# Four-layer kernel, layer 3: expert groups finish their tokens and scatter rows to the output, and blank slots are written behind the tokens

## The chip, the cores and the metric

The kernel runs on one core of a Trainium2 chip. The metric is the device time of one execution in microseconds (us); the figure used is the median of the runs shown. Engine names: PE is TensorE (matmul; PEld its weight loads), DVE is VectorE, ACT is ScalarE, POOL is GpSimd, SP is SyncE, which here only issues DMAs. "Idle" and "busy" are those of the profile.

## What is computed

The input is 32 sequences of 256 tokens with 128 numbers each: 8192 tokens, which the kernel holds as 64 tiles of 128 tokens (one token a partition). Four layers of "x = x + mixer(norm(x))" and "x = x + feed-forward(norm(x))" follow. The change concerns mainly the last line of the last layer, and with it the slots that layer 1 uses too:

```python
# layer 1: 8 experts, 2 a token, hidden size 512, gelu, plus one shared expert
# layer 3, feed-forward part (x is the normed stream, 8 experts, one a token, hidden size 256)
attn_out = mha(x)                                   # 16 heads of 8
x = layernorm(x + attn_out, ln1_g, ln1_b)
gp = softmax(x @ w_group + b_group)                 # group of experts
ep = softmax(x @ w_expert[group] + b_expert)        # expert in the group
moe = (g_prob * e_prob) * (relu(x @ w1[e] + b1[e]) @ w2[e] + b2[e])   # e: the one expert picked
x = layernorm(x + moe, ln2_g, ln2_b)
# and the stream's own residual around all of it: out = stream + x
```

## The kernel before, in words

**Stages in order of time.** Layer 0 (to about 830 us), layer 1 with its mixer, router and shared expert (to 1200), layer 1's routed experts (to 1490), layer 2's attention (to 2090), `middle` (layer 2's feed-forward and layer 3's recurrent mixer, to 2260), layer 3's attention with its router beside it (to 2831, router and scatter to 2877), layer 3's routed experts (to 3017), and a last pass over all tokens (to the end).

**Slots.** A token that goes to an expert is put into a slot, a row in device memory. `Slots` (L304) gives each of 8 experts room for 8192 + 256 rows. A row is `WIDE` = 130 numbers: 128 of x, the row that its result belongs to (column D), and its weight (column D + 1). `send` (L476) is one indirect DMA on POOL for a tile of 128 tokens: row i goes to the slot that the router counted out. Experts work on groups of 256 slots, and there are always `tokens / 256 + 8` groups (72 in layer 1, 40 in layer 3), so slots without a token are also read. For these `fill` (L324), called in layer 0 (L962), writes all 67,584 rows of each layer with blanks, in 176 DMAs on POOL, each after an iota that gives a blank slot a row of its own to put its result in. The tensor `back` therefore has a row for each slot, and behind them one for each token.

**The expert stage.** `experts` (L489) is a hand-made pipeline: PE, ACT, DVE and SP run in the order in which the code issues instructions, and POOL takes its own in order too. For each group g the loop issues `rise(g)` (first matmul and the activation of group g), `fetch(g + 1)` and `fall(g - 1)`.
- `fetch`: SP reads the group's first slot into a register (L509) and loads 256 rows (`xs`, L513); DVE reads the expert number (L516), copies that expert's weights and bias (L520, L522), casts the column of places (L524), PE transposes the rows (L527), DVE copies the result out of PSUM (`xT`, L529).
- `rise`: PE makes `hp` (L538), ACT the activation `h` (L544).
- `fall`: PE makes `o` (L552, L557), DVE multiplies by the weights (`y`, L563), and POOL scatters 2 tiles of 128 rows to `back` by indirect DMA (L484).

The tiles `xs`, `place`, `b2`, `xT` and `y` have 4 buffers each, `w` and `h` have 3. `place` and `y` are free again when the scatter that reads them has landed.

**Layer 3 around it.** The tile `row` (L2352) holds all 64 tiles of layer 3 for the whole layer, 130 numbers a token; `middle` borrows its memory as scratch. `attention` (L1643) works on 32 sequences b in 4 steps each (step t, 128 steps plus a lead of 7 and an end of 4), in the order written in `step`. `rows(b)` (L2420) writes the normed input of sequence b, 4 sequences ahead; `done(b)` (L2581) takes the statistics of the attention's sum and adds the last norm's offset to `K.x`. Every 8 tiles (`CHUNK`, 4 sequences) a generator `settle` (L2434) applies the norm, on POOL except for the last chunk; `gate` (L2453) transposes a pair of tiles and makes its router logits, once in 4 steps (`t % TURNS == 2`), and at each step from 128 on; `choose` (L2489) picks the expert, counts out slots (`places`, L378) and sends 8 tiles. `beside` advances each generator by one step, twice in a step t; only the oldest `choose` moves. After the last step `more(None)` runs what is left. `finish` (L434) works out the expert and first slot of each group.

**The last pass** (L2631 to L2665). In four quarters of 16 tiles: SP loads results from `back` (L582), DVE adds them (L2639) and takes statistics (L246), `Norm.steps` (L252, 19 small DVE instructions) closes the norm, ACT applies mean and scale (L2648), DVE multiplies by the norm's gain (L2655), POOL adds the stream (L2656), SP writes the output (L2657).

Of the kernel before, what the change touches and what calls it, by code (L numbers as in the profile page):

```python
# [11 lines left out]
F32 = mybir.dt.float32  # L12
# [8 lines left out]
P = 128  # L21
# [203 lines left out]
class Norm:  # L225
# [18 lines left out]
    def take(self, src, lo, hi):  # L244
        for j in range(lo, hi):
            self.nc.vector.bn_stats(self.st[:, j, :], src[:, j, :])  # L246
# [57 lines left out]
class Slots:  # L304
# [8 lines left out]
    GROUP, WIDE, NE = 256, D + 2, 8  # L313
    ROOM = NT * P + GROUP

    def __init__(self, K, es, tag, ranks):
        self.K, self.tag, self.ranks = K, tag, ranks
        self.groups = ranks * NT * P // self.GROUP + self.NE
        self.count = self.NE * self.ROOM
        dram = K.pool(es, tag + "slots", 1, DRAM)  # L320
        self.rows = dram.tile([self.count, self.WIDE], F32, name=f"{tag}_rows")
        self.back = dram.tile([self.count + ranks * NT * P, D], F32, name=f"{tag}_back")

    def fill(self, pool):  # L324
        nc = self.K.nc
        n = 6
        blank = [pool.tile([P, n, self.WIDE], F32, name=f"blank{i}") for i in range(2)]
        for t in blank:
            nc.gpsimd.memset(t, 0.0)
        rows = self.rows.rearrange("(c p n) w -> c p n w", p=P, n=n)  # L330
        for i in range(self.count // P // n):
            t = blank[i % 2]
            nc.gpsimd.iota(  # L333
                t[:, :, D], pattern=[[1, n]], base=i * n * P, channel_multiplier=n,
                allow_small_or_imprecise_dtypes=True,
            )
            nc.gpsimd.dma_start(rows[i], t)  # L337

    def begin(self, pool, most):

        nc = self.K.nc
        self.every = pool.tile([P, P], BF16, name="every")
# [28 lines left out]
    def belongs(self, row, j, n, rank):  # L371

        self.K.nc.gpsimd.iota(
            row[:, j : j + n, D], pattern=[[P, n]], base=self.count + (rank * NT + j) * P,
            channel_multiplier=1, allow_small_or_imprecise_dtypes=True,
        )

# [56 lines left out]
    def finish(self, pool, long, expert, start):  # L434
# [16 lines left out]
        past = pool.tile([1, n, NE - 1], F32, name="past")  # L451
        nc.vector.tensor_tensor(
            past, self.number.unsqueeze(2).to_broadcast([1, n, NE - 1]),
            end[0:1, 0 : NE - 1].unsqueeze(1).to_broadcast([1, n, NE - 1]), ALU.is_ge,
# [3 lines left out]
        nc.vector.tensor_scalar(expert, which, float(long), None, ALU.mult)  # L458
# [3 lines left out]
            past, past, need[0:1, 0 : NE - 1].unsqueeze(1).to_broadcast([1, n, NE - 1])  # L462
# [20 lines left out]
    def result(self, place, row):  # L483
        i = self.K.nc.gpsimd.indirect_dma_start(  # L484
            self.back, bass.IndirectOffsetOnAxis(ap=place, axis=0), row, None
# [3 lines left out]
    def experts(self, w_all, expert, start, F, act):  # L489
# [9 lines left out]
        with ExitStack() as ps:  # L499
            gp = K.pool(ps, tag + "g", 4)  # L500
            wp = K.pool(ps, tag + "gw", 3)
# [5 lines left out]
            def fetch(g):  # L507
# [4 lines left out]
                xs = gp.tile([P, N, self.WIDE], F32, name="xs")  # L512
                nc.sync.dma_start(  # L513
                    xs, self.rows[bass.ds(at, self.GROUP)].rearrange("(n p) w -> p n w", p=P)
                )
                at = nc.vector.value_load(  # L516
# [6 lines left out]
                place = gp.tile([P, N], mybir.dt.uint32, name="place")  # L523
                nc.vector.tensor_copy(place, xs[:, :, D])  # L524
# [4 lines left out]
                nc.vector.tensor_copy(xT, t)  # L529
# [19 lines left out]
            def fall(g):  # L549
# [12 lines left out]
                y = gp.tile([P, N, D], F32, name="y")  # L562
                nc.vector.tensor_mul(y, o, xs[:, :, D + 1 : D + 2].to_broadcast([P, N, D]))  # L563
                for i in range(N):
                    self.result(place[:, i : i + 1], y[:, i, :])

            with K.tc.manual_schedule(
                engines={nc.tensor.engine, nc.scalar.engine, nc.vector.engine, nc.sync.engine}
            ):
                for g in range(-1, self.groups + 1):  # L570
# [4 lines left out]
                    if g > 0:  # L575
                        fall(g - 1)

    def results(self, pool, n, eight):

        back = self.back[self.count :].rearrange("(r j p) d -> r p j d", r=self.ranks, p=P)  # L580
# [331 lines left out]
def l0_ffn(K):  # L912
# [4 lines left out]
    with ExitStack() as es:  # L917
# [44 lines left out]
        for slots in (K.slots1, K.slots3):  # L962
            slots.fill(sp)
# [675 lines left out]
RING = 4  # L1639
# [1139 lines left out]
```

## Time and profile before

| what | value |
|---|---|
| median of 4 runs | 3089.6 us (3083.45 to 3095.86) |
| the profiled execution, its own time | 3094.01 us |
| its span, first to last instruction | 3092.3 us |
| busy: PE, DVE, ACT, POOL | 2492.2, 1853.7, 1424.5, 854.4 us |
| layer 3's experts, first load to last scatter | 2877.0 to 3018.5 us |
| scatters of results (L484) | 224, 958 ns each (median) |
| scatters of rows (L478) | 192, 958 ns each (median) |
| blank DMAs (L337) and iotas (L333) | 176 each, 557 and 136 ns (median) |

The profile is of one execution. Its chain of waits follows the work that ended last back to its releaser. A row of groups names line, engine, operation, output and input, count, busy time, mean of one, then idle time before it and what ended that. "SPq" and "DVEq" are the instruction queues' own work, such as issuing a DMA or loading a register.

### The profile page before, as it was taken

To read this page: it belongs to the slowest core of one execution; us is meant where nothing else is said; L and a number is where in the kernel's file an instruction comes from. 1 tells how busy PE (TensorE), PEld (TensorE's weight loads), DVE (VectorE), ACT (ScalarE), POOL (GpSimd) and SP (SyncE) were. 2 spreads that over 40 slices of the span, in tenths; PEclk is the share of its full clock that TensorE was granted. 3 is DMA by queue.
4 is the path that set the end of the run, shared out by engine and by line. 5 is a ranking of instruction groups with operands and counts; after the bars stand their busy time and mean duration, and the time that the engine had idled before them with its cause. 6 is when DMAs were issued, how large, how long until landed. Compare 5 with 4: busy or idle time off the path is not lost.

```text
span 3092.3 us, 59293 instructions
## 1 busy us (share of the span) xinstructions
PE 2492.2 (81%) x21486; PEld 1848.1 (60%) x21486; DVE 1853.7 (60%) x5498; ACT 1424.5 (46%) x3065; POOL 854.4 (28%) x1235
## 2 busy tenths in 40 slices
PE   4899778899797953999489989997978888886670
PEld 4865444445766742999466767766755555564560
DVE  7215444445877312444389767755879988886347
ACT  3423432222387521444345555556337776664223
POOL 1001444310012455455311001000620234334553
PEclk9999889999898986999779999996979999998795
DMA  2497455530001111222455444420044445440324
GB/s 71 142 283 221 180 237 225 223 131 18 12 1 56 39 42 51 70 70 70 121 159 160 126 126 140 137 61 12 1 117 133 137 126 142 125 140 28 90 74 112
DMA packets 263264, 340.81 MB, mean 110 GB/s; under 512 B 34598, under 2 KB 231062, under 8 KB 254780
## 3 DMA queue, kind: packets, MB, share of 16 engines
q1 hardware_dynamic: 231228, 237.01, 26.8%
q0 software_dynamic: 27584, 97.92, 8.4%
q8 instruction: 170, 2.79, 0.4%
q10 hardware_dynamic: 4160, 2.10, 0.3%
q14 instruction: 122, 1.00, 0.1%
HBM read 156.72 MB, written 177.83 MB: 108 GB/s over the span
## 4 chain that ended last, share of the span: by engine, by line
PE 39%; DVE 11%; issue 7%; DMA 5%; POOL 5%; ACT 5%; SPq 1%; another core or an unknown queue 0%; POOLq 0%; ACTq 0%; DVEq 0%
PE o L1909 6%; PE t L1888 5%; PE hp L538 4%; PE o L557 4%; DVE top L1845 4%; DMA q<-row 3%; PE s L1784 2%; PE s L1833 2%; POOL f_back L484 2%; PE a L1592 2%; PE d L1607 2%; ACT e L1896 2%; DVE st_x L246 1%; POOL f_rows L478 1%; PE a L1492 1%
## 5 line engine op out<-in xcount | busy, mean ns | idle before, releaser
L1845 DVE TENSOR_REDUCE top<-s 128x3 f32<-128x384 f32 (+1 forms) x1024 | 600.3, 617 | 177.6 <-PE s L1742 122.6
L1896 ACT ACTIVATE e<-t 128x384 f32<-128x384 f32 (+1 forms) x1024 | 493.8, 546 | 121.6 <-PE s L1742 78.7
L1888 PE MATMUL t<-q,k 64*128 64x256 f32 (+1 forms) x2048 | 421.3, 310 | 108.7 <-ACT e L1896 62.3
L1833 PE MATMUL s<-k,q 48*128 48x256 f32 (+1 forms) x2048 | 441.6, 333 | 28.4 <-DMA k<-d 16.1
L1888 PEld LDWEIGHTS t<-q,k 64*128 64x128 f32 x2048 | 303.2, 193 | 188.8 <-ACT e L1896 91.1
L1833 PEld LDWEIGHTS s<-k,q 48*128 48x128 f32 x2048 | 311.3, 200 | 42.0 <-DVE top L1845 22.6
L544 ACT ACTIVATE h<-hp,w 128x256 f32<-128x256 f32 x368 | 154.4, 471 | 356.5 <-PE hp L538 304.5
L484 POOL DMA_INDIRECT f_back<-y,place x224 | 216.8, 968 | 216.1 <-DVE y L563 146.3
L1909 PE MATMUL o<-e,val 128*32 128x256 f32 (+1 forms) x4096 | 260.2, 374 | 0.0
L538 PE MATMUL hp<-xT,w 128*128 128x256 f32 x736 | 188.9, 397 | 30.2 <-DVE xT L529 23.2
L557 PE MATMUL o<-w,h 128*128 128x128 f32 x1472 | 187.6, 280 | 0.0
L557 PEld LDWEIGHTS o<-w,h 128*128 128x128 f32 x1472 | 178.5, 197 | 1.8
L2079 POOL TENSOR_SCALAR xn<-x_sb,mean_x,r_x 128x128 f32<-128x128 f32 x64 | 55.1, 869 | 441.3 <-PE t L1773 386.4
L538 PEld LDWEIGHTS hp<-xT,w 128*128 128x128 f32 x736 | 135.9, 197 | 50.6 <-DVE xT L529 27.1
L1909 PEld LDWEIGHTS o<-e,val 128*32 128x32 f32 x4096 | 110.2, 112 | 81.1 <-issue 11.2
L1742 PE MATMUL s<-hideq,pick 64*128 64x128 bf16 x1024 | 153.1, 235 | 0.0
L478 POOL DMA_INDIRECT f_rows<-row,one x128 | 123.3, 963 | 101.9 <-DVE one L1422 67.6
L1742 PE MATMUL t<-hidek,pick 64*128 64x128 bf16 x1024 | 148.7, 229 | 0.0
L527 PE MATMUL t<-ident,xs 128*128 128x128 f32 x224 | 45.4, 286 | 105.3 <-DMA xs<-f_rows 105.3
L563 DVE TENSOR_TENSOR y<-o,xs 128x256 f32<-128x256 f32 x112 | 47.4, 423 | 129.6 <-PE o L557 116.2
L337 POOL DMA_DIRECT2D f_rows<-blank x176 | 98.4, 559 | 54.5 <-POOL blank L333 51.2
L775 PE MATMUL up<-wc,hT 128*128 128x128 f32 x768 | 110.8, 297 | 0.0
(522 smaller groups left out, 5297.3 us busy)
## 6 DMA issues: line engine op xcount, KB each, us to landing
f_rows<-blank POOLq DMA_DIRECT2D x176, 390.0 KB
tz<-kpad SPq DMA_DIRECT2D x64, 512.0 KB
d<-high SPq DMA_DIRECT2D x128, 256.0 KB
d<-low SPq DMA_DIRECT2D x128, 256.0 KB
q<-d SPq DMA_DIRECT2D x128, 256.0 KB
k<-d SPq DMA_DIRECT2D x128, 256.0 KB
xs<-f_rows SPq DMA_DIRECT2D x112, 130.0 KB
t<-f_back SPq DMA_DIRECT2D x24, 512.0 KB
```

The lines of the kernel that those rows point to most:

```text
L478: i = self.K.nc.gpsimd.indirect_dma_start(self.rows, bass.IndirectOffsetOnAxis(ap=slot, axis=0), row, None)
L484: i = self.K.nc.gpsimd.indirect_dma_start(self.back, bass.IndirectOffsetOnAxis(ap=place, axis=0), row, None)
L538: nc.tensor.matmul(hp[:, i, :], w[:, (c + i) * P : (c + i + 1) * P], xT, start=True, stop=True,)
L544: nc.scalar.activation(h[:, c + i, :], hp[:, i, :], act, bias=w[:, b1 : b1 + 1])
L557: nc.tensor.matmul(o[:, i, :], h[:, c, i * P : (i + 1) * P], w[:, F + c * D : F + c * D + D], start=False, stop=i == N - 1 and c == FC - 1,)
L775: nc.tensor.matmul(o, hT[:, 2 * blk + b, s : s + P], wc[:, j, cs], start=j == 0, stop=False)
L1742: nc.tensor.matmul(t.rearrange("p (n q) -> p n q", n=3)[:, 0:3:2, 64 * n : 64 * n + 64], pick[r, n, :], hide[name][r], start=False, stop=n ...
L1833: nc.tensor.matmul(s[:, lo:hi], q[r, p, h * P : (h + 1) * P], k[r, p, 0 : hi - lo], start=h == 0, stop=not causal and h == 1,)
L1845: nc.vector.tensor_reduce(tops[b][:, :, j, p], out_of["s"][:, 0:used].rearrange("q (h k) -> q h k", h=3 if causal else 2), axis=AX.X, op=A ...
L1888: nc.tensor.matmul(t[:, kh * SEQ : kh * SEQ + SEQ - skip], k[r, p, kh * P : (kh + 1) * P], q[r, p, skip:SEQ], start=kh == 0, stop=not caus ...
L1896: nc.scalar.activation(e, t, AF.Exp)
L1909: nc.tensor.matmul(o[32 * i : 32 * i + 32, skip:SEQ], val[b % RING][:, kh, 4 * m + i, 16 * s : 16 * s + 32], e[:, kh * SEQ : kh * SEQ + SE ...
```

## The change

- A slot row of layer 3 has 258 numbers: the token's normed x, the stream's row with the last norm's offset already added, place and weight. Layer 1's rows stay at 130. `row` becomes a ring of 18 tiles of two token tiles each, one a sequence.
- Expert groups of layer 3 finish their tokens in a new `leave`: product with the weight plus x, statistics, and, for four groups at a time, the norm's closing, its application, gain and sum with the stream; then the row is scattered straight to the kernel's output. Work is metered: 11 units an iteration, 1 for a small DVE instruction, 5 for a group. The last pass is gone.
- `xs`, `place` and the new result tile have 12 buffers in layer 3 (4 in layer 1 as before). In layer 3 the copy `xT` moves from DVE to ACT.
- `fill` is gone. `begin` writes one blank group, and `blanks` writes 256 blank rows behind each expert's last token (SP reads the position from a tile into a register). A blank's place lies outside the output, and the scatter leaves out places that are out of bounds. The first group's load waits for the blank writes.
- One group fewer in both layers (71 and 39).
- Layer 3's `gate` runs every second step; `middle` has a scratch tile of its own.

The core of the diff:

```diff
 class Norm:
+    def take(self, src, lo, hi, at=None):   # statistics of src[at...] to column lo...
 class Slots:
-    GROUP, WIDE, NE = 256, D + 2, 8
+    GROUP, NE = 256, 8
+        self.PLACE, self.WEIGHT, self.WIDE = width, width + 1, width + 2
-        self.groups = ranks * NT * P // self.GROUP + self.NE
+        self.groups = self.tokens // self.GROUP + self.NE - 1
...
+    def put_blank(self, at):
+        i = self.K.nc.sync.dma_start(
+            self.rows[bass.ds(at, self.GROUP)].rearrange("(n p) w -> p n w", p=P), self.blank
+        )
+    def blanks(self, pool):
+        nc.vector.tensor_copy(last, self.seen[0:1, :])
+        for e in range(self.NE):
+            self.put_blank(
+                nc.sync.value_load(
+                    last[0:1, e : e + 1], min_val=0, max_val=self.count - self.GROUP
+                )
+            )
...
     def result(self, place, row):
-            self.back, bass.IndirectOffsetOnAxis(ap=place, axis=0), row, None
+            self.back, bass.IndirectOffsetOnAxis(ap=place, axis=0), row, None,
+            bounds_check=self.tokens - 1, oob_is_err=False,
...
     # experts(..., leave, keep, copy)
+            kp = K.pool(ps, tag + "gk", keep)
-                xs = gp.tile([P, N, self.WIDE], F32, name="xs")
+                xs = kp.tile([P, N, self.WIDE], F32, name="xs")
-                nc.vector.tensor_copy(xT, t)
+                copy(xT, t)
-                y = gp.tile([P, N, D], F32, name="y")
-                nc.vector.tensor_mul(y, o, xs[:, :, D + 1 : D + 2].to_broadcast([P, N, D]))
-                for i in range(N):
-                    self.result(place[:, i : i + 1], y[:, i, :])
+                leave(g, o, xs, place)
...
 def l0_ffn(K):
-        for slots in (K.slots1, K.slots3):
-            slots.fill(sp)
...
 def layer1(K):   # in choose, after places; leave there is the old product and two scatters
+            if hi == NT:
+                S.blanks(rw)
...
 def l3_ffn(K):
+                row_of[b] = kept.tile([P, 2, S.WIDE], F32, name="row")   # kept: 18 buffers
-                nc.vector.reciprocal(row[:, lo:hi, D + 1], low)
+                for j in range(lo, hi, 2):
+                    two = row_of[j // 2]
+                    nc.vector.reciprocal(two[:, :, S.WEIGHT], low[:, j - lo : j - lo + 2])
+                    S.belongs(two, j, 2, 0)
-                two = K.x[:, 2 * b : 2 * b + 2, :]
-                nc.gpsimd.tensor_add(two, two, spread(2, 3))
+                nc.gpsimd.tensor_add(
+                    row_of[b][:, :, D : 2 * D], K.x[:, 2 * b : 2 * b + 2, :], spread(2, 3)
+                )
-                if t % TURNS == 2 or t >= NB * TURNS:
+                if t % 2 == 0 or t >= NB * TURNS:
...
+            def out_of(g, j, r, xs, place):
+                for i in range(2):
+                    nc.scalar.activation(
+                        r[:, i, :], r[:, i, :], AF.Identity, bias=nmr[:, j + i : j + i + 1],
+                        scale=first.r[:, j + i : j + i + 1],
+                    )
+                nc.vector.tensor_mul(r, r, spread(2, 2))
+                nc.gpsimd.tensor_add(r, r, xs[:, :, D : 2 * D])
+                for i in range(2):
+                    S.result(place[:, i : i + 1], r[:, i, :])
+            def work(groups):
+                lo, hi = groups[0][1], groups[-1][1] + 2
+                for _ in first.steps(lo, hi):
+                    yield 1
+                nc.vector.scalar_tensor_tensor(
+                    nmr[:, lo:hi], first.mean[:, lo:hi], -1.0, first.r[:, lo:hi], ALU.mult, ALU.mult
+                )
+                yield 1
+                for group in groups:
+                    out_of(*group)
+                    yield 5
+            def leave(g, o, xs, place):
+                if g is not None:
+                    j = g // BATCH % SETS * tiles + 2 * (g % BATCH)
+                    r = yp.tile([P, 2, D], F32, name="r")
+                    for i in range(2):
+                        nc.vector.scalar_tensor_tensor(
+                            r[:, i, :], o[:, i, :], xs[:, i, S.WEIGHT : S.WEIGHT + 1],
+                            xs[:, i, 0:D], ALU.mult, ALU.add,
+                        )
+                        nc.vector.bn_stats(first.st[:, j + i, :], r[:, i, :])
+                    batch.append((g, j, r, xs, place))
+                if batch and (g is None or g % BATCH == BATCH - 1 or g == S.groups - 1):
+                    todo.append(work(batch[:]))
+                    batch.clear()
+                most = 11 if g is not None else 1000
+                while todo and most > 0:
+                    done = next(todo[0], None)
...
+            S.experts(w_all, expert, start, F, AF.Relu, leave, 3 * BATCH, nc.scalar.copy)
-        # the last pass: results, join, close, end
```

## The prediction

> **What bounds the kernel now.** I read the slices first, then the waits stage by stage, then the chain from 2840 us on, and last the timeline of single groups. The windows around the change (PE, PEld, DVE, ACT, POOL busy; granted clock; DMA share; GB/s):
>
> ```profile
> 2264.00:2831.00 567.00, 479.46 (x4958) 324.36 (x4958) 480.11 (x1366) 377.03 (x836) 161.64 (x212) 0.95 0.44 125
> 2831.00:2877.00 46.00, 6.55 (x30) 5.37 (x30) 23.65 (x123) 6.54 (x34) 23.25 (x24) 0.50 0.28 81
> ...
> 2888.00:3017.50 129.50, 96.81 (x577) 83.58 (x575) 54.64 (x188) 31.86 (x76) 76.85 (x79) 0.91 0.27 78
> 3017.50:3092.30 74.80, 0.00 (x0) 0.00 (x0) 57.29 (x168) 25.06 (x64) 26.86 (x17) 0.50 0.41 114
> ```
>
> In the attention (567 us) PE and DVE are each 85% busy. From 2831 to 2877 nearly everything waits. In the experts' 129.5 us no engine is full (PE 75%, POOL 59%, DVE 42%). In the last 74.8 us PE has nothing to do: this pass stands alone at the end. The chain of waits says what holds these stretches:
>
> ```profile
> 2873.37 0.96 POOL f_rows L478
> 2874.33 14.00 issue
> ...
> 2990.01 1.27 issue
> 2991.51 0.96 POOL f_back L484
> ...
> 3019.81 4.12 DMA t<-f_back
> ...
> 3073.87 11.07 POOL x_sb L2656 x7
> ```
>
> The experts hang on POOL's scatters, and still POOL idles: one scatter is 0.96 us and 0.30 us to the next, so two are 2.52 us a group, while 40 groups took 129.5 us, 3.24 each. The waits of 2886 to 3017 us name the missing part: places waiting for scatters to land, POOL waiting for the product.
>
> ```profile
> POOL f_back L484 <- DVE y L563: 44.2, 18, 14.2
> ...
> DVE place L524 <- DMA f_back<-y,place: 16.1, 7, 3.7
> ```
>
> This is the ring of 4 places and products: the product of one group waits for a landing, the next scatter waits for the product.
>
> **Part 1, the last pass goes into the groups.** I count DVE per group, from starts in the timeline:
>
> ```profile
> 2920.08 0.43 DVE L520 COPY w<-w_all 128x514 f32 x1 [0.45 <-issue]
> 2920.42 0.22 DVE L522 CAST b<-w_all 128x128 bf16 x1
> ...
> 2924.14 0.16 DVE L524 CAST place<-xs 128x2 uint32<-128x2 f32 x1
> ```
>
> - Weights 0.34 to the next start, bias 0.13, place 0.17: 0.64. Before the weights DVE loads the expert's register: a gap of 0.43 typically (0.10 where its queue ran ahead); I take 0.43. The copy `xT` (0.42) goes to ACT.
> - Two products with sum, 128x128: L1562, the same instruction in layer 1, means 344 ns, 0.68. Two statistics: eight take 1.65 us (L246), 0.42.
> - The closing of a norm: 20 instructions, 3029.76 to 3033.70, 3.94 us; once per four groups, 0.99 each. The gain: L2447 on DVE, 128x256, 0.43 and a step of 0.03: 0.46.
> - Sum 3.62 us. Waits on ACT: after the closing, two Identities (64 in 25.1 us, 0.39 each) and two hand-overs before the first gain, 1.0 us; the three other gains follow ACT's 0.78 instead of 0.46, 1.0 more. Two per batch, 0.50 each: 4.1.
> - The gain against POOL's addition: L2655 (128x512) takes 684 ns at its fastest and 1660 at the median, with POOL adding beside it. The addition fills 0.72 of some 4 us, so I add 0.1: **c = 4.2 us a group**.
>
> [...] If each group's gain met the addition of the group ahead and waited half of it, 0.36 instead of 0.1, the sum below would be 9 us longer.
>
> The other engines stay under 4.2: POOL 2 x 1.26 + 0.72 (L2585, the same addition of 128x256) + 0.06 = 3.3; PE 2.36 (start to start of transposes, 2891.27 and 2893.63); ACT 2 x 0.42 + 0.37 + 0.78 = 2.0. Twelve buffers instead of four take away the wait for landings: a place waits for the scatter 12 groups back, and POOL has at least 4 groups queued then. So what is late next is DVE, in its own order. SP is queued behind nothing new here; a load is 0.9 us of its queue (L509 and L513: 0.27 + 0.15 + 0.02 + 0.04 + 0.03 + 0.38), and rows of 264 KB instead of 130 come 12 groups ahead.
>
> The stretch from the first load of slots to the end of the span is 3092.3 - 2877.0 = 215.3 us now. After: 10.9 us to the first product (2877.0 to 2887.9, PE cold, unchanged); three more groups with no work given out, 2.6 each (PE's 2.36, a little slower at the start), 7.8; 35 groups at 4.2, 147.0; then the last batch: nine closing steps 1.9, Identities and gain 1.5, POOL's three groups 9.9, the last landing 2.3 (3017.51 to 3019.81) and 1.4 to end, 17.0. Together 182.7: **-32.6**.
>
> Ends for c: 3.3, POOL's sum, if DVE's waits vanish; 5.2, if PE runs cold (below). An output row lands like a row of `back` now: both are 512 bytes.
>
> **Part 2, the stretch before.** `gate` twice as often finishes a chunk's logits 8 steps earlier (4 pairs in steps 30 to 36 instead of 30 to 42, the fifth gate at 38 instead of 46). So the sixth chunk's sends, 2834.80 to 2844 now, fall into the attention; the seventh's `choose` starts at about 2831 instead of 2836; the last one no longer waits for it until 2853.84 but starts when its logits are there, 2849.80. From there to slots took 6.7 us, then eight sends at 1.26: the last ends at 2867 instead of 2874.3, -7.4. But now SP writes blanks: eight register loads and DMAs at 0.95, 7.6 us, from when all tokens are counted (2859.4 now, about 2855.4 then), sharing its queue with the 17 weight loads (2855.9 to 2864.5); and the first slots wait for these 2.1 MB. That ends at 2870 to 2874, as a load lands in 2.1 us (2876.99 to 2879.09), against 2877.0 now. I take **-5**; from -7.4 to +5, if the weights queue behind the blanks.
>
> **Part 3, the attention.** The first `rows` now stand at 2209 us, before `middle` ends. The ring lies over `middle`'s memory, so they wait for its last matmul, as `xT` does today (2258.82, released by L2324): four Identities at 0.45 and a transpose on the way, **+3** (0 to 4). The ring itself: a sequence's row is sent at steps 49 to 52 of its chunk's count and overwritten at step 56, 4 to 7 steps of 4 us later; a scatter lands in 2.3. No stall. 24 more reciprocals on DVE, 0.16 to 0.20 each, 4.3 us on an engine that is 85% busy: **+3** (0 to 5). 32 iotas (0.14) and no more additions than before lie on POOL, 29% busy here; rows of 1032 bytes instead of 520 leave POOL's 0.96 a send as it is, or double it at worst: for the last eight sends alone +8.
>
> **Part 4, elsewhere.** Layer 1 has one group fewer, at 3.84 us (1484.92 to 1481.08, PE-bound): **-3.8**. Its scatters go the new bounded way: 2.52 of 3.84 us, hidden at today's price. The 176 blank DMAs and their iotas take 122 us of POOL and most of the DMA traffic of 340 to 640 us, but in 320 to 700 us only one compute wait of note names a DMA, `xn` L991 for 9.6 us, and it ends at 340.17, when DVE finishes `nmr` at 340.0 anyway. So **0**, from -5 to 0. Two small blank fills at the layers' starts (0.4 us of POOL, one DMA issue) hide behind DVE's norm and bias splitting.
>
> **Sum**: -32.6 - 5 + 3 + 3 - 3.8 = -35.4. The profiled execution took 3094.0 (span 3092.3 and 1.7 around it), 4.4 over the median; I take the difference from the median: 3089.6 - 35.4 = **3054**.
>
> **Rivals.**
> 1. *PE goes cold and DVE's order tightens* (0.17). While DVE closes a norm, ACT stands at the Identity, and the next `h` behind it on ACT waits; PE then runs out. For: after 2.43 us idle PE's four matmuls took twice as long:
>
> ```profile
> 2913.22 2.08 PE L538 MATMUL hp<-xT,w 128*128 128x256 f32 x4 [2.43 <-DVE xT L529]
> ...
> 2916.91 1.03 PE L538 MATMUL hp<-xT,w 128*128 128x256 f32 x4
> ```
>
> Against: it recovered by the next group, and PE may run a group ahead. A cold group is 4.7 us; with hand-overs c = 5.0 gives -7.4: 3082. [...]
> 2. *POOL sets the pace* (0.12): ACT and DVE hide each other's waits, c = 3.3: -35.4 - 35 x 0.9 = -67: 3023. For: POOL would hold some groups of work ahead, so DVE's waits cost it nothing; against: DVE's bare sum is already 3.6.
> 3. *The bounded scatter is dearer, slower* (0.08). No row has one. At x us each, layer 1 is POOL-bound above 1.92, and 71 (2x - 3.84) + 35 (2x + 0.78 - 4.2) reaches the 35.4 gained at x = 2.02. At 2.2 it is slower by 39: 3129. For: 1792 or so blank rows a layer have to be left out; against: the work per row is a comparison.
> 4. *The ring of 18 stalls ACT* (0.04): if sends fell back to today's step 57, after the overwrite at 56, each of 14 sequences would wait some 4.5 us: +63, 3117.
>
> That the last pass remains in some form is excluded by the code.
>
> **Chances.** My forecast (c from 3.6 to 4.8, 3033 to 3075) has 0.59, rivals 0.17, 0.12, 0.08 and 0.04. About 0.5% (15 us) is what a measurement can tell from no change. Faster by more: forecast, rival 2 and a little of rival 1: 0.73. Within: the rest of rival 1, 0.14. Slower: rivals 3 and 4 and the far end of 1, 0.13. The range leaves out rivals 3 and 4 and the ends of 1 and 2: 3024 to 3088.
>
> **What would show it.** Right: no DVE or POOL work after the last `o` but some 17 us; in the expert stage DVE over 80% busy, 4.2 us between transposes, no place waiting for a scatter; `f_rows` loads from about 2874; the bounded scatter at 0.96 us. Wrong: `hp` at twice its length in most groups; POOL above 90% there; a scatter above 1.9 us in layer 1; ACT waiting for `f_rows` in the attention; a stage before 700 us that got shorter.

## The result, and the profile after

The changed kernel took **3079.8 us** (median of 44 runs, 3065.0 to 3097.1), the kernel before 3086.8 on the same chips (70 runs, 3071.1 to 3100.9); the ratio is 0.9974 [0.9964, 0.9983]. The sign was forecast, the size was not: -7.0 us by the medians, instead of -35.4. The profiled execution after took 3081.93, its span 3080.2, 12.1 less than the span before.

The same windows as before, with ends set by the same events (columns: PE, PEld, DVE, ACT, POOL busy; granted clock; DMA share; GB/s). The third is two full batches of the experts, the fourth begins with the last `o`:

```profile
2264.00:2831.00 567.00, 494.85 (x4960) 334.15 (x4960) 483.25 (x1392) 376.81 (x842) 164.62 (x241) 0.94 0.45 129
2831.00:2882.50 51.50, 6.38 (x30) 5.25 (x29) 21.16 (x117) 4.23 (x24) 20.91 (x22) 0.52 0.44 141
2928.00:2963.00 35.00, 21.69 (x120) 18.73 (x120) 27.30 (x105) 14.86 (x41) 22.54 (x25) 0.89 0.32 92
3048.00:3080.20 32.20, 1.29 (x8) 1.04 (x8) 9.53 (x35) 5.70 (x15) 18.68 (x21) 0.55 0.06 17
```

The last pass with 74.8 us of no PE work is gone; 32.2 us remain, and POOL is the busy engine in them. DVE is 78% busy in the experts (27.30 of 35; the sign asked for over 80%), POOL 64%. But the stretch of waiting after the attention has grown, from 46.0 to 51.5.

The account, step by step, with ends read from the timelines. The rows on `rows` and on the attention are means over all profiles with the one code or the other in that stage (four before, but three for the attention, where `b_gate2` has code of its own, and thirteen after), since single executions scatter there by 4 to 8 us; the others are of the pair of profiles. (In that pair alone the attention ends 0.7 us later after, where the first three rows add up to 5.8; hence 12.1 between the two spans and 7.0 between the medians.)

| step | forecast | measured |
|---|---|---|
| layer 1, one group fewer (first to last `hp`, 275.1 to 271.2) | -3.8 | -3.9 |
| `rows` waits for `middle` (last addition of layer 2 to first of layer 3, 237.9 to 239.6) | +3 | +1.7 |
| layer 3's attention (first to last addition of the joined stream, 498.8 to 506.8) | +3 | +8.0 |
| Part 2, last addition to first load of slots (47.0 to 51.8) | -5 | +4.8 |
| Part 1, first load to the end of the span (215.3 to 197.7) | -32.6 | -17.6 |
| stages without the fill | 0 | not to be told from 0 (below) |
| sum | -35.4 | -7.0 |

So the 28.4 us that are missing lie in three places: 15.0 in Part 1, 9.8 in Part 2 and 3.7 in the attention and its start. Part 1 once more, by its own terms:

| | forecast | measured |
|---|---|---|
| first load to the end of the first `o` | 10.9 | 11.6 |
| to the end of the last `o`, 38 intervals | 154.8 | 155.9 |
| end of the last `o` to the end of the span | 17.0 | 30.2 |

**The pace was right, the end was not.** The timeline of the end of the experts:

```profile
3048.68 1.29 PE L588 MATMUL o<-w,h 128*128 128x128 f32 x8 [0.86 <-ACT h L575]
3048.81 0.68 POOL L2699 TENSOR_TENSOR r<-r,xs 128x256 f32<-128x256 f32 x1 [3.76 <-DVE r L2698]
...
3049.77 1.00 POOL L501 DMA_INDIRECT out<-r,place  x1 [0.28 <-POOL r L2699]
...
3061.76 0.71 POOL L2699 TENSOR_TENSOR r<-r,xs 128x256 f32<-128x256 f32 x1
...
3070.42 0.98 POOL L501 DMA_INDIRECT out<-r,place  x1 [0.30 <-issue]
```

When PE makes the last product, POOL only begins the batch before it: four groups with eight scatters, 3048.81 to 3061.76, 12.95 us. Then come the last three groups, 9.64 us to 3071.40, which the forecast had (9.9), and 8.8 us to the end of the span. The last closing and its Identities (forecast 1.9 and 1.5) lie hidden beside the work on those four groups. POOL's closing step, a DRAIN in the profile, takes up nearly all of the 8.8; its rows after, and then before:

```profile
L2845 POOLq DRAIN  x3: 51/116/11945, 3067.5 to 3079.9; - x3
L2845 SPq DRAIN  x3: 7/7/7, 3072.8 to 3079.7; - x3
L2775 POOLq DRAIN  x3: 46/116/7528, 3084.0 to 3092.0; - x3
```

Columns are shortest, median and longest in ns, first and last start. SP, which waits for the last data, begins to close at 3072.8; POOL's long step begins at 3067.5, lasts 11.9 us and so ends at 3079.4, 8.0 us after its last scatter. In before the same step ended 5.4 us after POOL's last instruction, an addition.

**The rhythm behind it**, in the chain of waits through the experts (start, length, what):

```profile
2937.34 0.98 POOL out L501
...
2940.96 3.67 issue
...
2958.20 4.21 issue
```

Here POOL has emptied its queue and waits, once a batch (17.35 us for four groups, 4.35 a group). It waits because DVE closes the norm only behind the fourth product, and it gets four groups at once:

```profile
2943.05 0.17 DVE L2707 SCALAR_TENSOR_TENSOR nmr<-mean_x,r_x 128x8 f32<-128x8 f32 x1
2943.25 0.88 ACT L2694 ACTIVATE r<-r,nmr,r_x 128x128 f32<-128x128 f32 x2 [5.47 <-DVE nmr L2707]
...
2944.16 0.43 DVE L2698 TENSOR_TENSOR r<-r,b_f_ln 128x256 f32<-128x256 f32 x1 [0.94 <-ACT r L2694]
...
2944.67 0.67 POOL L2699 TENSOR_TENSOR r<-r,xs 128x256 f32<-128x256 f32 x1 [3.72 <-DVE r L2698]
...
2945.78 1.75 PE L569 MATMUL hp<-xT,w 128*128 128x256 f32 x4 [3.21 <-DVE b L553]
```

POOL works 13.6 us and idles 3.7. In the body its idle time costs nothing, since DVE sets the pace; but the batch is handed on so late that its whole work is still to do when the next batch's products end.

**The stretch before the experts.** The chain of waits there:

```profile
2860.66 0.71 issue
2861.39 0.71 SPq L375
2862.09 0.70 issue
2862.82 0.71 SPq L388
2863.52 0.70 issue
2864.24 0.70 SPq L375
...
2874.12 0.37 SPq L375
2874.53 0.27 SPq L388
2874.85 0.15 SPq L388
2875.26 0.37 SPq L375
...
2876.83 0.47 SPq L2677
...
2882.50 2.62 DMA xs<-f_rows
```

SP writes the blanks (L375 issues the DMA, L388 loads the register). From 2860.66 each of its small steps, or the pause ahead of it, takes 0.70 us, and only at 2872.7 do they return to 0.37 and less, some 3 us after the last scatter of rows began (2869.61). The eight blanks take 15.4 us instead of the forecast's 7.6, and 8 of the 17 weight loads queue behind them, from 2876.83.

### The profile page after: what moved, and what is told of

The parts are those of the page before. It is cut to its first block, busy times and chain, and to the rows that moved or that the text cites. A ratio compares the mean times of both kernels' runs of the same rounds, so it can differ in the third digit from the quotient of the medians.

```text
span 3080.2 us, 59477 instructions
## 1 busy us (share of the span) xinstructions
PE 2513.2 (82%) x21444; PEld 1865.2 (61%) x21444; DVE 1872.4 (61%) x5663; ACT 1437.0 (47%) x3112; POOL 739.4 (24%) x933
## 5 line engine op out<-in xcount | busy, mean ns | idle before, releaser
L1930 PE MATMUL t<-q,k 64*128 64x256 f32 (+1 forms) x2048 | 427.5, 312 | 93.5 <-ACT e L1938 45.5
L569 PE MATMUL hp<-xT,w 128*128 128x256 f32 x724 | 190.2, 404 | 51.6 <-DVE b L553 32.3
L495 POOL DMA_INDIRECT f_rows<-row,one x192 | 185.9, 968 | 181.0 <-DVE one L1451 67.1
L501 POOL DMA_INDIRECT f_back<-y,place x142 | 141.4, 996 | 143.5 <-DVE y L1665 99.7
L1951 PEld LDWEIGHTS o<-e,val 128*32 128x32 f32 x4096 | 110.6, 113 | 82.0 <-issue 12.9
L551 DVE COPY w<-w_all 128x1028 f32 (+1 forms) x110 | 74.1, 674 | 67.8 <-DVE y L1665 29.2
L558 PEld LDWEIGHTS t<-ident,xs 128*128 128x128 f32 x220 | 33.2, 152 | 126.2 <-issue 115.3
```

The costliest lines, as they stand in the source:

```text
L495: i = self.K.nc.gpsimd.indirect_dma_start(self.rows, bass.IndirectOffsetOnAxis(ap=slot, axis=0), row, None)
L501: i = self.K.nc.gpsimd.indirect_dma_start(self.back, bass.IndirectOffsetOnAxis(ap=place, axis=0), row, None, bounds_check=self.tokens - 1, ...
L569: nc.tensor.matmul(hp[:, i, :], w[:, (c + i) * P : (c + i + 1) * P], xT, start=True, stop=True,)
L1930: nc.tensor.matmul(t[:, kh * SEQ : kh * SEQ + SEQ - skip], k[r, p, kh * P : (kh + 1) * P], q[r, p, skip:SEQ], start=kh == 0, stop=not caus ...
L1951: nc.tensor.matmul(o[32 * i : 32 * i + 32, skip:SEQ], val[b % RING][:, kh, 4 * m + i, 16 * s : 16 * s + 32], e[:, kh * SEQ : kh * SEQ + SE ...
```

## The experiments

Marks used below: "stretch" is the last addition of the attention to the first load of slots (before 47.03, after 51.82), "body" the first to the last `hp` (before 130.2, after 158.7), "tail" from there to the end of the span (81.7 and 35.2), "stage" first load to end (215.3 and 197.7). Each ratio is to the kernel before, run in turn on the same chip. `a_fill3_again`, `b_gate2` and `c_nofill` ran on a chip on which the kernel before took 3096.0 us, so their times compare with others only by the ratio. Stretch, body, tail and stage are of one profile each.

**The ring, in the kernel before (`b_keep12`).** Three pools get 12 buffers in layer 3:

```diff
+            kp = K.pool(ps, tag + "gk", 12 if self.ranks == 1 else 4)
-                xs = gp.tile(...); place = gp.tile(...); y = gp.tile(...)
+                xs = kp.tile(...); place = kp.tile(...); y = kp.tile(...)
```

> The kernel before with one edit: in layer 3's expert stage the tiles xs, place and y have 12 buffers instead of 4. Theory (the step of part 1 that says a ring of 4 places and products holds POOL back): 40 groups go from 3.24 us to POOL's two scatters, 2.52 to 2.6 us, so the stage is 25 us shorter and the time some 3062 us. Rival (the product comes late for another reason, the chain of copy, product and activation through DVE, ACT and PE): the pace stays near 3.2 us and the time near 3087 us.

3086.1 us, ratio 1.0003 [0.9982, 1.0024]; 3.22 us a group, 3.32 in the kernel before. Its longest waits in the experts:

```profile
ACT h L545 <- PE hp L539: 37.2, 16, 3.5
POOL f_back L484 <- DVE y L564: 22.5, 13, 2.3
```

No place waits for a landing any longer, POOL's wait for the product has halved (44.2 before), and the pace is the same within the scatter (body 126.3 for 130.2; in `b_gate2`, with these groups unchanged, 124.0). "This is the ring of 4" falls: the wait was there, but it did not hold the pace.

**The same with `xT` on ACT (`b_keep_xT`)**: `nc.scalar.copy` at L529 as well.

> The kernel before, with 12 buffers for xs, place and y in layer 3 (which alone changed nothing: 3.22 us a group instead of 3.32) and the copy xT on ACT as in the changed kernel. Theory (DVE's order is what holds the groups: the copy xT stands behind weights, bias and place and ahead of the product): the pace falls to 2.6 us, POOL's two scatters, and the time by some 20 us to 3065. Rival (the loop of PE and ACT, or stalls that no engine explains): the pace stays above 3.0 us and the time within 5 us of before.

3085.1 us, 0.9997 [0.9976, 1.0017], body 130.05. So neither the ring nor DVE's copy held the old experts; what does stays open. Of the change it says that the deeper rings, alone or with `xT` moved, bring nothing.

**Blanks filled early again (`a_fill3`, and a second time `a_fill3_again`).** Layer 3's slots are filled in layer 0 by 88 DMAs from one constant tile, nothing is written behind the tokens:

```diff
+    def fill(self, pool): ...; for i in range(self.count // P // n): nc.gpsimd.dma_start(rows[i], blank)
+        K.slots3.fill(sp)
-                if hi == NT:
-                    S.blanks(rw)
```

> The changed kernel, but layer 3's slots are filled with blanks in layer 0 (88 DMAs on POOL, 70 MB, all with a place outside the output), and no blanks are written behind the tokens of layer 3. Theory (SP's eight register loads and blank writes, with half the weights queued behind them, set the start of the experts): the first slots load at 2873.5 to 2875 us instead of 2882.5, the time falls by 8 us against the changed kernel. Rival 1 (the start hangs on the router's last scatters and the weights themselves): no change, within 2 us. Rival 2 (the fill in layer 0 is not free): 5 us or more are lost before 830 us.

> The kernel with the fill in layer 0 once more, since its trace had 10.6 us less ahead of the experts than the changed kernel and its median only 3. If the trace is right, the median is now 3067 to 3071; if the fill costs something ahead of 2830 us that one profile can't show, 3075 to 3078 again.

3076.7 us, 0.9962 [0.9946, 0.9979], and 3078.9, 0.9938 [0.9917, 0.9959]. The stretch is 41.2 and 41.1: 10.6 shorter than after, 6 shorter than before. The first load comes 2.9 us after the last scatter of rows, where after has 12.9. So in the profiles the blanks behind the tokens cost 10.6 us of the stretch. The times show less of it: by the ratios 4 us and 11 us below after, the first not clear of noise. The second run's 3078.9 is what its expectation gave for a fill that costs something elsewhere, but by the ratio, on the median of the kernel before, it would be 3068, which is what the profile says; layer 1 starts no later with the fill (below).

**What slows SP.** Three kernels were run once, one in turn with the kernel before. `a_nosend` fills early, writes the blanks too and leaves out the last chunk's eight scatters (its tokens don't reach the experts). `a_now` loads only expert 0's weights and the biases, three loads (the other experts' are zeros; the expectation's count of ten is a slip). `a_wact` issues the weights from ACT. `a_wfirst` puts the blanks behind all weight loads on SP.

```diff
# a_nosend
-                    S.send(one, row(j))
+                    if hi < NT: S.send(one, row(j))
# a_now
+            nc.gpsimd.memset(w_all[:, :, 0 : 2 * F], 0.0)
-            for e in range(NE):
+            for e in range(1):
# a_wact
-                nc.sync.dma_start(w_all[:, e, 0:F], ins["f3_w1"][e])
+                nc.scalar.dma_start(w_all[:, e, 0:F], ins["f3_w1"][e])
# a_wfirst: S.blanks moved behind the loop of loads
```

> The changed kernel, with layer 3's slots also filled in layer 0, and without the last chunk's eight scatters of rows (these 1024 tokens are left out). For the 0.70 us that each SP instruction takes ahead of and among the blank writes. Theory 1 (POOL's scatters of rows slow SP while they run): SP goes at its usual pace, the eight blanks take 9.3 us instead of 15.4. Theory 2 (the weights' traffic) and theory 3 (first use of these instructions after a long time): 0.70 us each remain for 9 to 12 us.

> The changed kernel, loading the first product's weights of one expert only, and all second products' weights (the other experts' first weights are zeros that POOL writes, some 4 us more on POOL ahead of its scatters). Theory 2 (weights in flight on SP's queue slow its other instructions): with ten loads instead of 17 and five of the nine ahead of the blanks gone, the stretch of 0.70 us instructions shrinks by half or vanishes. Theories 1 and 3: it stays, and by theory 1 it ends some 3 us after the last scatter of rows, wherever that is.

> The changed kernel with layer 3's 17 weight loads issued on ACT's queue instead of SP's. So far SP's instructions took 0.70 us each only where the weights were loaded on SP and rows were scattered by POOL at once: not without the last scatters, and not with 3 loads instead of 17. If SP's own loads are what matters, SP goes at its usual pace here: eight blanks in 9.3 us, and from the attention's last addition to the first slots load 51.8 us become 43 to 46. If the traffic matters whoever issues it, the 0.70 us steps remain and it stays over 49.

> The changed kernel with layer 3's blanks issued on SP after the 17 loads of the weights instead of after 9 of them. Theory (order on SP's queue: the weights' second half waits behind the blanks, whose register instructions take 0.7 us each for 12 us): the weights are issued by 2864 us, the blanks then end at 2874 to 2877 and the first slots load at 2876 to 2879 instead of 2882.5: the time falls by 4 to 6 us. Rival (the slow SP instructions are due to the place behind a long wait, so they only move): the blanks end at 2881 and nothing is gained, within 2 us.

SP's row of the eight blanks in the timeline of each (start, time from the first to the last one's end). After:

```profile
2861.39 15.40 SPq L375 DMA_DIRECT2D f_rows<-blank  x8
```

`a_nosend`, no last scatters:

```profile
2863.16 8.54 SPq L385 DMA_DIRECT2D f_rows<-blank  x8
```

`a_now`, three loads:

```profile
2850.14 8.78 SPq L375 DMA_DIRECT2D f_rows<-blank  x8
```

`a_wact`, loads issued by ACT:

```profile
2849.83 17.29 SPq L375 DMA_DIRECT2D f_rows<-blank  x8
```

`a_wfirst`, blanks last on SP:

```profile
2865.21 9.28 SPq L375 DMA_DIRECT2D f_rows<-blank  x8
```

Without the scatters the blanks take 8.5 us; with the scatters but nearly no weights 8.8; with both, and the weights issued by ACT (`a_wact`), 17.3, for 15.4 in after (stretch 50.5, for 51.8). So, by single profiles, the slow steps need both the scatters and the weight loads, and it is not SP's own queue that matters.

But the two kinds of traffic need not run at the same time, and where they do SP can be fast. First the kernel before, 2868 to 2876 us, where the weights have landed and only the queue of the scatters moves data, and one of SP's steps there; then the two queues of `a_now`, 2853 to 2859 us, while its blanks go at full pace:

```profile
q0 software_dynamic: 192, 0.40, 14.9%
L509 SPq FUSED_REGOPS  x1: 709/709/709, 2873.4 to 2873.4; - x1
...
q1 hardware_dynamic: 1357, 1.32, 65.6%
q0 software_dynamic: 158, 0.45, 23.7%
```

So what the weight loads leave behind that slows SP, and why a step that moves no data takes 0.70 us, stays open. In `a_wfirst` the blanks come after the slow steps, which now lie ahead of them: its stretch is 51.6, time 3080.3, 0.9984 [0.996, 1.0007]. Nothing is gained by the order. Without the last scatters, or with three loads, the stretch is 44.4 (`a_nosend` and `a_now`; the latter also spares SP fourteen loads). As an estimate from `a_nosend`, of the 10.6 us some 7.4 are the slow steps and 3.2 the blanks themselves; `a_fill3` has slow steps ahead of its first load too, so this split is rough. The single executions (`a_nosend`, `a_now`, `a_wact`) took 3075.8, 3064.3 and 3068.7 us; the executions of one kernel lie up to 32 us apart (after), so these times decide nothing.

**Batches of eight (`a_batch8`)**: `BATCH, SETS = 8, 4` instead of `4, 4`, so the norm is closed half as often.

> The changed kernel with BATCH 8 instead of 4 (a norm is closed for eight groups; rings of 24). Theory (DVE sets the pace of 4.32 us a group, and 1.0 of it is a quarter of a closing): the pace falls to 3.8 us, 39 groups save 17 to 19 us; POOL gets a longer backlog at the end, which gives back up to 8: the time falls by 10 us, between 5 and 18. Rival (ACT's waits or POOL set the pace): the pace stays above 4.2 us and the time within 3 us, or longer by what the last batch's seven groups add on POOL.

3071.1 us, 0.9945 [0.9922, 0.9968]. Body 139.8, 18.9 shorter, 0.50 a group: half of the closing's 0.99, as the DVE-bound sum says. The tail is 10.7 longer (up to 8 was expected), the stage 8.2 shorter. The first and last `hp`, after and then `a_batch8`:

```profile
L569 PE MATMUL hp<-xT,w x156: 379/382/796, 2886.4 to 3045.1; 128*128 128x256 f32 x156
L569 PE MATMUL hp<-xT,w x156: 379/379/796, 2886.0 to 3025.8; 128*128 128x256 f32 x156
```

Both parts of the theory hold: DVE sets the body, and the tail is what POOL has left to do.

**The last additions on DVE (`a_tail`, `a_tail2`).** The sum with the stream moves from POOL to DVE: in `a_tail` for what is left when the loop has ended, in `a_tail2` from group 36 on.

```diff
+                e = nc.vector if over[0] else nc.gpsimd
-                nc.gpsimd.tensor_add(r, r, xs[:, :, D : 2 * D])
+                e.tensor_add(r, r, xs[:, :, D : 2 * D])
+                over[0] = g is None          # a_tail2: g is None or g >= 36
```

> The changed kernel, but in the final flush (all that is left after the last group's product) DVE adds the stream's row instead of POOL. Theory (behind the last product POOL has seven groups to do, not three: four of the batch before and the last three, at 3.24 us each, two scatters and an addition): some six to seven additions of 0.67 us leave POOL, so from the last first product (2 matmul groups ahead of the end) to the end of the span 35.2 us become 30 to 31. Rival (the closing on DVE and the 8.8 us from the last scatter to the end of the span set it): under 1.5 us.

> The changed kernel, with DVE adding the stream's row from group 36's turn on, thus for six or seven of the last seven groups (the run before had it for the last three alone, since the batch before them is worked off in the last group's turn, and gained 1.9 us of tail). Theory (POOL works off seven groups behind the last product): 0.65 us for each, so from the last first product to the end 30.5 to 31.3 us instead of 35.2. Rival (DVE's last closing sets the end): no less than 33.

`a_tail`: 3078.7 us, 0.9976 [0.9961, 0.9991], tail 33.3, 1.9 less, which the time doesn't show (0.9974 after). Only three groups' additions moved, since the batch before them had been issued by then: 3 x 0.65. `a_tail2` (a single execution, 3065.3 us): 31.3, 3.9 less; seven groups' additions moved, and 3.9 is what six cost POOL at 0.65. The first of them in the timeline:

```profile
3035.27 0.43 DVE L2700 TENSOR_TENSOR r<-r,xs 128x256 f32<-128x256 f32 x1
```

What remains is 14 scatters at 1.29 us, one after the other on POOL.

**`gate` twice as often, in the kernel before (`b_gate2`)**: `t % 2 == 0` instead of `t % TURNS == 2`.

> The kernel before with one edit: gate at every second step instead of every fourth, as in the changed kernel, and nothing else. For the two halves of what it moves. Theory (the sixth chunk's choice and scatters are moved into the attention and paid there on DVE, which is 85% busy): the attention of layer 3 lasts 503 to 505 us instead of 497 to 501, and from its end to the first slots load 40 to 42 us instead of 47: together a gain of 0 to 2 us. The forecast's view: 7.4 us less behind the attention and nothing in it, a gain of 7.

3093.7 us, 0.9994 [0.9973, 1.0016]. The stretch is 40.9, 6.1 shorter, nearly what Part 2 said (-7.4); but the attention took 502.3, 3.5 over the mean of the kernel before (three profiles, 497 to 501). So work moved into the attention seems to be paid for there, by about half of what it saves. One profile does not show that firmly, and the interval of the ratio leaves room for a gain of 8 us.

**Put together.** `c_best1` is `a_fill3`, batches of eight and the last additions on DVE; `c_nofill` the same with blanks behind the tokens; `c_best2` is `c_best1` with batches of 8, 8, 7, 6, 4, 4, 2, no metering from group 36 on, and DVE's additions from 33.

> The changed kernel with three edits together: layer 3's blanks filled in layer 0 (none behind the tokens), BATCH 8, and the final additions on DVE. If they add up as the traces had them alone (first slots load 10.4 us earlier behind the attention's end; from the first slots load to the end 8.2 us less; the tail 4 to 5 less), the time is 22 to 23 us below the changed kernel's 3080: 3057. Rival (what the medians had: 3 for the fill, 9 for the batch, and some of the tail): 3065. If POOL is now the bound of the stage, the tail's saving is the whole of its seven additions.

> The kernel that took 3054, but with the blanks written behind the tokens on SP as in the changed kernel (BATCH 8 and the last additions on DVE stay). Theory (the blanks cost what the traces say: from the attention's last addition to the first slots load 51.8 us with them, 41.2 to 41.8 without): 10 us more, 3064, between 3060 and 3068. Rival (the medians of the fill alone: 3 us): 3057.

> The kernel with the fill in layer 0, BATCH 8 and the final additions on DVE, further changed: batches of 8, 8, 7, 6, 4, 4 and 2 groups, no metering from group 36 on, and DVE's additions from group 33 on. Theory (POOL's backlog behind the last product is what is left): two more closings cost DVE up to 8 us where it has them to spare late, six more additions leave POOL (4 us), and the last batch is two groups instead of seven: the end comes 4 to 8 us earlier than 3054. Rival (DVE is the bound up to the last product): 0 to 5 us later.

`c_best1`: **3054.1 us**, 0.9883 [0.986, 0.9906], the fastest here, 26 below after and 33 below before (by the ratio 36). Stretch 41.8, stage 182.1: 10.1 and 15.6 less than after, 25.7 in all. `c_nofill` takes 3073.1, 0.9924 [0.9901, 0.9947]: 0.0041 or 13 us more, by intervals that overlap at their ends; its stretch is 53.0, which is 11.2 longer. The time itself lies outside its expectation (3060 to 3068); by the ratio, on the median of the kernel before, it would be 3063. `c_best2`: 3054.3, 0.991 [0.9879, 0.994]. Its tail falls to 28.7 (`c_best1` 40.9), but its body rises from 137.3 to 149.9. Two more closings, at 3.94 us each in the prediction's count, are some 8 us of that; the rest was not separated. The stage is 182.5. What the tail gives back the body takes.

## Why the prediction was right in sign and wrong in size

**Part 1, the pace: right.** 4.35 us a group for 4.2, DVE-bound; `a_batch8` confirms the closing's share. The reading of the old groups that went with it, the ring of 4, was wrong (`b_keep12`), but no term of the sum stood on it. POOL's and PE's sums stayed under it: in the groups of the experts after, PE was cold about once a batch (11 of 39 `hp` at 1.75 us or more), not in each.

The contention term was 0.1 and measured more, in another place too. Two rows of groups of after, 2893 to 3045 us:

```profile
L551 DVE COPY w<-w_all 128x514 f32 x36 | 23.0, 640 | 14.0 <-issue 14.0
L2698 DVE TENSOR_TENSOR r<-r,b_f_ln 128x256 f32<-128x256 f32 x32 | 16.9, 570 | 7.8 <-ACT r L2694 7.8
```

The gain's mean is 570 ns against the prediction's 430 (+0.14; a wait of half an addition would have been 0.36), and the weight copy, which was left out, 640 against the 430 of the prediction's row (+0.21).

**Part 1, the tail: wrong; this is the largest failed step.** "the last batch: nine closing steps 1.9, Identities and gain 1.5, POOL's three groups 9.9, ... 17.0" let POOL be empty when the last batch came. It has a whole batch to work off, 12.95 us, of which 11.8 lie behind the end of the last `o`, and behind the last scatter 8.8 us pass, not 3.7. With the closing and the Identities hidden (3.4) and the three groups shorter by 0.3, that makes the 13.2 by which 30.2 is over 17.0. The prediction itself held the fact that it needed: POOL "has at least 4 groups queued then" and "would hold some groups of work ahead".

**Part 2: wrong.** The "eight register loads and DMAs at 0.95, 7.6 us" took 15.4. The rate was taken from the expert stages, where POOL scatters results group after group but the weights have long been loaded. The far end, +5 "if the weights queue behind the blanks", was met (+4.8), but by luck: eight of the weight loads did stand behind the blanks, and yet with all of them ahead (`a_wfirst`) the stretch is 51.6. What the sum lacked is SP's slow steps. The two halves, measured apart, are -6.1 (`b_gate2`) and +10.6 (`a_fill3`), together +4.5.

**Part 3: low.** The wait for `middle` is there, +1.7 for +3; `row`'s wait in after, ACT idle 3.2 us for `middle`'s last product, is the one named. The attention grew by 8.0 for 3: the reciprocals took 2.6 of DVE's time, within what was forecast, but the chunk that moved forward was costed at nothing, and `b_gate2`, by its one profile, gives 3.5. The rest, about 2, was not separated.

**Part 4: right** for layer 1 (-3.9) and the bounded scatter (rival 3). For the fill, layer 1's first `hp` stands at 1210 to 1214 us with the code before and 1209 to 1216 with the changed one: it cost nothing before, and so gave nothing.

**Rivals.** *PE cold* came in part, at c 4.35 and not 5.0. *POOL sets the pace*: no in the body, yes in the tail, where the prediction had not looked for it. *The bounded scatter is dearer*: no; layer 1's scatters of results take 983 ns for 958:

```profile
L501 POOL DMA_INDIRECT f_back<-y,place x142: 980/983/1496, 1225.3 to 1493.6; - x142
```

*The ring of 18 stalls ACT*: no wait of ACT for a send was found.

## What to carry to other kernels

When a pass is folded into a pipeline, ask what each engine still has in its queue when the last item enters: a batched step hands its work on a batch late, and that batch is paid for in full at the end. Take the price of an instruction from a stretch with the same work around it, not merely the same instruction. Work moved forward into a stage whose engines are 85% busy can be paid there in part (3.5 of 6.1 us in `b_gate2`, by its one profile): measure the stage that receives it.

## What the runs showed of the hardware that was not expected

- **SP's steps of 0.70 us.** Register loads, moves and waits on SP, 0.02 to 0.37 us elsewhere, take 0.70 (or the pause ahead of them does) while POOL scatters rows and the weights are being loaded or have just been. It is in the kernel before as well (2865 to 2876.95, so its first load came 3.6 us after its last scatter began), and in `a_fill3`. The cause stays open.
- **POOL's closing step** lasts until 8.0 us after the last scatter ended, though the data had landed by 3072.8. From the end of the last scatter to the end of the span it is 8.8 to 8.9 us in after, `a_batch8`, `a_tail`, `a_tail2` and `a_wfirst`, but 7.3 to 7.4 in `a_fill3` and `c_best1`, which have the fill in layer 0 and end on the same scatter; so part of this end goes with the program, and the fill saves some 1.5 us here as well. Why is open.
- **A copy meets POOL as well.** In the timeline of after:

```profile
2951.60 1.04 DVE L551 COPY w<-w_all 128x514 f32 x1 [0.48 <-issue]
2951.63 1.54 POOL L2699 TENSOR_TENSOR r<-r,xs 128x256 f32<-128x256 f32 x2
...
2957.40 0.43 DVE L551 COPY w<-w_all 128x514 f32 x1 [1.03 <-issue]
```

 With POOL adding beside it, it takes 1.04 us instead of 0.43. A small two-input instruction of DVE (L437, 128x8), 0.17 us by its median in after, took 2.07 us once in `a_batch8` (2624.90), beside two additions of POOL (2624.96 and 2625.60, 0.67 us each). Why is open.
- **The clock.** In the experts after, `hp` took 2.04 to 2.05 us three times after 3.25 us idle, and 1.10 after 2.44 (twice), 2.87 and 3.05; but 2.04 also after 2.97 and 2.19, and 1.38 after 3.26. So the length of one idle time does not decide. In the trace of after, from 2895 to 3000 us, the granted clock keeps one value for 3.41, 6.83, 10.24, 13.65 or 17.07 us at a time, that is one to five windows of 3.41 us. Two such windows before, with the prediction's row of 2.08 us in the second, and then three windows after (columns as above):

```profile
2909.51:2912.93 3.42, 1.28 (x12) 1.07 (x10) 0.26 (x2) 0.84 (x2) 1.92 (x2) 1.00 0.34 101
2912.93:2916.34 3.41, 3.12 (x10) 2.60 (x11) 1.62 (x6) 0.84 (x2) 2.04 (x2) 0.50 0.22 61
...
2939.27:2942.68 3.41, 2.32 (x15) 2.00 (x15) 2.73 (x14) 0.00 (x0) 1.38 (x2) 1.00 0.12 40
2942.68:2946.10 3.42, 0.32 (x2) 0.32 (x3) 2.06 (x8) 2.85 (x8) 1.15 (x2) 1.00 0.00 0
2946.10:2949.51 3.41, 3.41 (x15) 2.96 (x14) 3.34 (x9) 2.42 (x7) 2.83 (x4) 0.50 0.41 116
```

 After 1.28 and 0.32 us of PE work the next window has half the clock, after 2.32 the full one. In the profiles of before and after, from 2880 to 3000 us, 10 windows at full clock were followed by one at half, with PE busy for 0.32 to 1.35 us of each, and 38 by another at full clock, with PE busy for 1.49 us or more. The prediction's 2.43 us without PE (2910.79 to 2913.22) lie with 2.14 us in the first of the two windows before, which had 1.28 us of PE work besides.
